# A recurrent block with a mixture of experts: the last expert's order, the residual loads and the closing additions

## The chip, the cores and the metric

The kernel runs on one core of a Trainium2 chip. The core has a matrix engine (PE, whose weight loads are listed apart as PEld), a vector engine (DVE), a scalar engine (ACT), GpSimd (POOL), a queue engine that here only issues DMAs (SP), and 16 DMA engines. The metric is the device time of one execution in microseconds (us). Times inside an execution are counted from the start of its span, that is, from the first to the last instruction.

## The reference

The input is x, 8192 tokens of 256 float32 values. What is computed, cut to what matters here:

```python
xn = layernorm(x)                       # per token
s  = recurrent(xn)                      # linear, gate, scan over time, linear: 8192 x 256
# mixture of experts on the same xn: 32 experts, 4 per token, at most 1280 tokens per expert
h   = silu(xe @ w1[e]) * (xe @ w3[e])   # xe: the tokens that were sent to expert e
out = (h @ w2[e]) * weight              # per slot
y   = zeros.at[token].add(out)          # scatter-add back to the tokens
z   = (silu(xn @ sw1) * (xn @ sw3)) @ sw2
return x + s * silu(y + z)
```

All of it is float32.

## The kernel before

**First stage (to about 390 us).** The tokens are taken in 8 rounds of 1024. Per round x is normalised, transposed, routed (top 4 of 32 experts by way of group maxima), projected by the recurrent part into `s_all`, which stays in SBUF (16 chunks of 128 partitions x 4 rows x 256), and sent row by row to the experts' slots in the DRAM table `xd_d` by indirect DMAs of POOL (`send`, L437). Two operations of this stage appear in the prediction: `recur` (L326), where DVE runs a scan over 8 x 1024 elements with two SBUF inputs (L333), and `scale` (L265), where POOL computes a power on 128 x 8 elements (L275). The shared expert z is computed here as well and stored to the DRAM table `y_d`.

**Expert stage (about 400 to 1226 us).** An expert's 1280 slots fall into three spans: two of 512 and a last one of 256. `load_slots` (L566) fetches a span from `xd_d`; `turn` (L576) transposes it on PE and computes the token numbers on DVE; `hidden` (L594, through `glu_hidden`, L113) does two matmul groups per half, a silu on ACT (L123) and a multiply on DVE (L124); `expert_out` (L597) multiplies by w2 on PE (L614), scales by the routing weight on ACT into `ob` (L617), and has POOL add each block of 128 rows to `y_d` by an indirect DMA with addition (L620, called a scatter below). `last_span` (L629) does the span of 256 under a condition: PE, DVE, ACT and POOL each load a flag and branch over it when an expert has no more than 1024 tokens.

The order on PE, DVE, ACT and SP is the program's own order (`manual_schedule`, L560); POOL is not among these engines, and its order is set by the scheduler, which puts the fourth scatter of span 0 behind the conditional span's two. The loop over experts (L646) is skewed: round e transposes and starts expert e while it finishes expert e - 1. One further round, e = 32, has no new expert; there only expert 31 is finished:

```python
            if old:
                hidden(e - 1, 1)
                expert_out(e - 1, 0)
            ...
            if old:
                last_span(e - 1)
            ...
            if old:
                expert_out(e - 1, 1)
```

Scatters of one expert go to different rows and do not wait for each other; the first of an expert waits until the last of the expert before it has landed.

**The residual chunks.** `load_residual` (L640) fetches a chunk of x into a tile `xr`. Thirteen of the sixteen are fetched in the expert stage, one after every second expert, into the pool `fin`. The other three are fetched after the stage into the pool `tail`, which takes over the SBUF space of the expert stage and so has to wait for the tiles that lay there.

**The tail (L671 on).** SP issues the 16 loads of `y_d` (y, 512 KB each). They need all scatters landed. Then for every chunk: a silu on ACT (L680), a multiplication by `s_all` on DVE (L681), an addition to `xr` on DVE (L682), and a store by SP (L683). SP issues its DMAs in program order over eight semaphores, and each DMA waits for the eighth before it to land; so the first store is issued when the ninth y load has landed.

Of the kernel before, what the change touches and what calls it, by code (L numbers as in the profile page):

```python
# [8 lines left out]
F32 = mybir.dt.float32  # L9
I32 = mybir.dt.int32  # L10
AF = mybir.ActivationFunctionType
ALU = mybir.AluOpType
# [4 lines left out]
def recurrent_moe_kernel(  # L17
# [18 lines left out]
    nc = tc.nc  # L36
    P = 128
    B, S, D = x.shape
# [12 lines left out]
    CT = 4  # L51
    CW = CT * P
    NC = N // CW
# [15 lines left out]
    out_f = out.rearrange("b s d -> (b s) d")  # L69
# [21 lines left out]
    s_all = keep.tile([P, NJ, D], F32, name="s_all")  # L91
# [5 lines left out]
    def apart(key, ins):  # L97

        tc.declare_no_dep(ins.ins, group=key, reason="different rows")
        tc.add_to_no_dep_group(key, ins.ins)  # L100

    def chunk(rows, c):

        r, h = divmod(c, RT // CT)
        return rows[r * TR : (r + 1) * TR, :].rearrange("(p j) d -> p j d", j=RT)[:, h * CT : (h + 1) * CT, :]

    def load_expert(e):
        w = wpool.tile([P, 3, KD, H], F32, tag="w", name=f"w_{e}")
        for i, src in enumerate((w1, w3, w2)):
            nc.sync.dma_start(out=w[:, i], in_=src[e].rearrange("(k p) h -> p k h", p=P))  # L110
        return w
# [15 lines left out]
    def transpose_in(src, j, p0, p1):  # L127

        for k, ps in enumerate((p0, p1)):
            nc.tensor.transpose(ps[:, j * P : (j + 1) * P], src[:, k * P : (k + 1) * P], ident)  # L130
# [4 lines left out]
    with tc.tile_pool(name="ab", bufs=1) as ab, tc.tile_pool(name="xp", bufs=4) as xp, tc.tile_pool(  # L135
        name="rt", bufs=2
# [31 lines left out]
        for i, src in enumerate((sw1, sw3, sw2)):  # L168
# [16 lines left out]
            out=tri, in_=tri, compare_op=ALU.is_gt, fill=0.0, base=0, pattern=[[1, P]], channel_multiplier=-1  # L185
# [18 lines left out]
            out=y_d[N : N + CAP, :].rearrange("(i p) d -> p i d", p=P),  # L204
            in_=hole[:, 0:D].unsqueeze(1).to_broadcast([P, EJ, D]),
# [293 lines left out]
        for r in range(NR + 1):  # L499
            new, old = r < NR, r > 0  # L500
            c = 2 * (r - 1)
# [54 lines left out]

    spans = [(i, min(CW, CAP - i)) for i in range(0, CAP, CW)]
    LAST = len(spans) - 1
    NX = NC - 3
    with tc.tile_pool(name="fin", bufs=NX, reuse_waits="tile") as fin, tc.manual_schedule(  # L560
        engines=engines
    ), ExitStack() as stack:
        mp = stack.enter_context(tc.tile_pool(name="moe", bufs=2, reuse_waits="tile"))
        ws, xes, rows, xTs, hTs = {0: first_w}, {}, {}, {}, {}

        def load_slots(e, i):  # L566
            s0, n = spans[i]
            xe = xes[e, i] = mp.tile(
                [P, n // P, XR], F32, tag=f"xe{n}", bufs=4 if n == CW else 2, name=f"xe_{e}_{s0}"
            )  # L570
            for j in range(n // P):
                q = s0 // P + j
                row0 = nc.sync.value_load(start[0:1, e, q : q + 1], min_val=FIRST - P, max_val=FIRST + E * EP - P)
                nc.sync.dma_start(out=xe[:, j, :], in_=xd_d[bass.ds(row0, P), :])

        def turn(e, i):  # L576

            s0, n = spans[i]
            m, j0 = n // P, s0 // P
            xe = xes[e, i]  # L580
            p0 = ps_tp.tile([P, CW], F32, tag="tp", name=f"ep0_{e}_{s0}")
            p1 = ps_tp.tile([P, CW], F32, tag="tp", name=f"ep1_{e}_{s0}")
            for j in range(m):
                transpose_in(xe[:, j, :], j, p0, p1)
            xT = xTs[e, i] = mp.tile([P, KD, n], F32, tag=f"xT{n}", name=f"xT_{e}_{s0}")
            nc.vector.tensor_copy(xT[:, 0, :n], p0[:, :n])  # L586
            nc.vector.tensor_copy(xT[:, 1, :n], p1[:, :n])  # L587
            row_f = mp.tile([P, CT], F32, tag="row_f", name=f"rf_{e}_{s0}")
            nc.vector.tensor_copy(row_f[:, :m], dump[:, j0 : j0 + m])
            nc.vector.copy_predicated(row_f[:, :m], used[:, e, j0 : j0 + m], xe[:, :m, XR - 1])  # L590
            row = rows[e, i] = mp.tile([P, CT], I32, tag="row", bufs=4, name=f"row_{e}_{s0}")
            nc.vector.tensor_copy(row[:, :m], row_f[:, :m])  # L592

        def hidden(e, i):  # L594
            hTs[e, i] = glu_hidden(mp, ws[e][:, 0], ws[e][:, 1], xTs.pop((e, i)), spans[i][1], f"{e}_{i}")

        def expert_out(e, i):  # L597

            s0, n = spans[i]
            w, xe, row, hT = ws[e], xes.pop((e, i)), rows.pop((e, i)), hTs.pop((e, i))  # L600
            ob = mp.tile([P, CT, D], F32, tag="ob", bufs=3, name=f"ob_{e}_{s0}")
            for j0 in range(0, n // P, 2):
                if n == CW:
                    po = ps_o.tile([P, 2, D], F32, tag="o", name=f"eo_{e}_{s0}_{j0}")
                    pos = [po[:, i, :] for i in range(2)]
                    order = [(m, i) for i in range(2) for m in range(KH)]
                else:
                    pos = [
                        ps_o.tile([P, 2, D], F32, tag="o", name=f"eo_{e}_{s0}_{j0 + i}")[:, 0, :] for i in range(2)
                    ]  # L610
                    order = [(m, i) for m in range(KH) for i in range(2)]
                for m, i in order:
                    tk = slice((j0 + i) * P, (j0 + i + 1) * P)
                    nc.tensor.matmul(pos[i], hT[:, m, tk], w[:, 2, m, :], start=(m == 0), stop=(m == KH - 1))  # L614
                for i in range(2):
                    j = j0 + i
                    nc.scalar.activation(ob[:, j, :], pos[i], AF.Copy, scale=xe[:, j, D + e : D + e + 1])  # L617
                    apart(
                        f"y{e}",
                        nc.gpsimd.indirect_dma_start(  # L620
                            out=y_d,
                            out_offset=bass.IndirectOffsetOnAxis(ap=row[:, j : j + 1], axis=0),
                            in_=ob[:, j, :],
                            in_offset=None,
                            compute_op=ALU.add,
                        ),
                    )

        def last_span(e):  # L629
            if (e, LAST) in xes:  # L630
                _, (more,) = nc.values_load_multi_w_load_instructions(  # L631
                    last[0:1, 0, e : e + 1], engines=(ET.PE, ET.DVE, ET.Activation, ET.Pool), min_val=0, max_val=1
                )
                with tc.If(more > 0):
                    hidden(e, LAST)
                    expert_out(e, LAST)

        xr = [None] * NC

        def load_residual(c, pool):  # L640
            xr[c] = pool.tile([P, CT, D], F32, tag="xr", name=f"xr_{c}")
            nc.sync.dma_start(out=xr[c], in_=chunk(x_f, c))

        for i in range(LAST + 1):
            load_slots(0, i)
        for e in range(E + 1):  # L646
            new, old = e < E, e > 0
            if new:
                turn(e, 0)
            if old:  # L650
                hidden(e - 1, 1)
                expert_out(e - 1, 0)
            if e + 1 < E:
                load_slots(e + 1, 0)
            if old:
                last_span(e - 1)
            if new:
                turn(e, 1)
                hidden(e, 0)
                turn(e, LAST)  # L660
            if old:
                expert_out(e - 1, 1)
            if e + 1 < E:
                ws[e + 1] = load_expert(e + 1)
                for i in range(1, LAST + 1):
                    load_slots(e + 1, i)
            if e % 2 == 1 and e // 2 < NX:
                load_residual(e // 2, fin)


        stack.close()  # L671
        tail = stack.enter_context(tc.tile_pool(name="tail", bufs=NC - NX, reuse_waits="tile"))
        for c in range(NX, NC):
            load_residual(c, tail)
        ys = []
        for c in range(NC):
            ys.append(tail.tile([P, CT, D], F32, tag="y", bufs=NC, name=f"y_{c}"))
            nc.sync.dma_start(out=ys[c], in_=chunk(y_d, c))
        for c, y in enumerate(ys):
            nc.scalar.activation(y, y, AF.Silu)  # L680
            nc.vector.tensor_tensor(y, y, s_all[:, c * CT : (c + 1) * CT, :], ALU.mult)  # L681
            nc.vector.tensor_tensor(xr[c], xr[c], y, ALU.add)  # L682
            nc.sync.dma_start(out=chunk(out_f, c), in_=xr[c])  # L683
# [1 line left out]
_INS = [  # L685
    "L0_attn_x",
# [35 lines left out]
```

## Time and profile before

| what | value |
|---|---|
| median of 3 runs | 1286.86 us (1284.95 to 1288.59) |
| the profiled execution: its time | 1286.5 us |
| the profiled execution: its span | 1284.8 us |
| mean granted PE clock | 0.958 |
| busy: PE | 1168.0 us (91%) |
| busy: DVE | 500.1 us (39%) |
| busy: ACT | 357.5 us (28%) |
| busy: POOL | 721.8 us (56%) |
| expert stage, 400 to 1226 us: PE busy | 812.5 us of 826.0 |
| from the last matmul to the first y load, 1226.0 to 1236.6 us: POOL busy | 7.2 us of 10.6 |
| tail, 1236.6 to 1284.8 us: DVE busy | 37.9 us of 48.2 |
| tail: DMA share, rate | 0.88, 348 GB/s |

The busy shares are averages over stages with different limits. The first two stages belong to PE; after 1226 us PE does nothing more, and 58.8 us of the span lie behind its last matmul. All that the change touches lies in or shortly before that end. A row of the timeline gives the start, the duration, the engine, the line, the operation and its tiles, and in brackets how long the engine was idle before it and what ended that idle time. In the chain of waits, each line is a piece of the work that ended last, in order of time: start, duration, engine, tile and line. Times on PE are modelled at the ends, and "issue" is time in which an engine waited for nothing that the profile shows.

### The profile page before, as it was taken

The numbers are of one execution on the slowest core, as the hardware profiler recorded it, in microseconds if no ns is written. First come the engines' busy times: TensorE is split into PE (matmuls) and PEld (weight loads), VectorE is DVE, ScalarE is ACT, GpSimd is POOL, SyncE is SP. The second block draws the span as 40 slices with busy tenths as digits, with TensorE's granted clock in tenths as the row PEclk, the third lists the DMA queues.
The fourth block names the chain that finished last, engine by engine and source line by source line (L and its number), as shares of the span: only waits on it lengthen the run. The fifth ranks groups of instructions, "written<-read, shape, count | busy, mean of one in ns | idle before, by whom it ended". The sixth has DMA issues, their size and how long they took to land. (4 is left out here: it accounts for less than half of the span.)

```text
span 1284.8 us, 15849 instructions
## 1 busy us (share of the span) xinstructions
PE 1168.0 (91%) x4246; PEld 733.7 (57%) x4246; DVE 500.1 (39%) x1591; ACT 357.5 (28%) x638; POOL 721.8 (56%) x561
## 2 busy tenths in 40 slices
PE   5599999999994999999999999999999999999910
PEld 3256565656552566666666656666666655665610
DVE  5765667564601322322223222332323232332238
ACT  2034433443320222222222222222222222222232
POOL 2477777777772355655545455545555545555630
PEclk9599999999996999999999999999999999999965
DMA  6134543433475476775776776758666767667488
GB/s 219 51 123 160 176 167 120 168 140 132 144 264 176 111 158 137 133 144 114 166 141 137 148 161 141 148 123 185 138 137 149 163 137 170 141 125 170 66 241 347
DMA packets 151251, 198.30 MB, mean 154 GB/s; under 512 B 17866, under 2 KB 134771, under 8 KB 151155
## 3 DMA queue, kind: packets, MB, share of 16 engines
q0 software_dynamic: 53184, 75.14, 30.8%
q1 hardware_dynamic: 95280, 120.01, 30.2%
q10 hardware_dynamic: 2690, 2.04, 0.5%
q8 instruction: 38, 0.62, 0.2%
q14 instruction: 59, 0.48, 0.1%
HBM read 99.05 MB, written 98.08 MB: 153 GB/s over the span
## 5 line engine op out<-in xcount | busy, mean ns | idle before, releaser
L620 POOL DMA_INDIRECT y_d<-ob,row x284 | 440.0, 1549 | 396.3 <-ACT ob L617 332.9
L440 POOL DMA_INDIRECT xd_d<-xt,put x256 | 263.7, 1030 | 94.0 <-issue 75.6
L95 PE MATMUL pa<-xT,w 128*128 128x512 f32 (+1 forms) x624 | 271.1, 557 | 0.0
L95 PE MATMUL pb<-xT,w 128*128 128x512 f32 (+1 forms) x624 | 269.3, 554 | 0.0
L614 PE MATMUL eo<-w,hT 128*128 128x256 f32 x1136 | 258.1, 379 | 0.1
L614 PEld LDWEIGHTS eo<-w,hT 128*128 128x128 f32 x1136 | 212.4, 190 | 42.9 <-issue 15.3
L617 ACT ACTIVATE ob<-eo,xe 128x256 f32<-128x256 f32 x284 | 120.0, 470 | 274.1 <-PE eo L614 229.7
L95 PEld LDWEIGHTS pb<-xT,w 128*128 128x128 f32 x624 | 118.7, 190 | 125.8 <-issue 122.9
L123 ACT ACTIVATE a<-pa 128x512 f32<-128x512 f32 (+1 forms) x156 | 87.2, 559 | 356.2 <-PE pa L95 343.0
L95 PEld LDWEIGHTS pa<-xT,w 128*128 128x128 f32 x624 | 114.2, 191 | 95.3 <-issue 92.4
L124 DVE TENSOR_TENSOR hT<-a,pb 128x512 f32<-128x512 f32 (+1 forms) x156 | 97.1, 638 | 162.2 <-PE pb L95 96.2
L592 DVE CAST row<-rf 128x4 int32<-128x4 f32 (+1 forms) x96 | 16.5, 172 | 270.7 <-DMA y_d<-ob,row 268.0
L586 DVE COPY xT<-ep 128x512 f32<-128x512 f32 (+1 forms) x96 | 57.6, 600 | 161.0 <-PE ep L130 161.0
L130 PE MATMUL ep<-ident,xe 128*128 128x128 f32 x640 | 89.7, 278 | 24.6 <-DMA xe<-xd_d 17.6
L130 PEld LDWEIGHTS ep<-ident,xe 128*128 128x128 f32 x640 | 75.0, 142 | 55.9 <-DMA xe<-xd_d 19.8
L95 PE MATMUL po<-Wio,xnT 128*128 128x256 f32 x256 | 71.7, 404 | 0.0
L95 PE MATMUL pa_s<-xnT,sw 128*128 128x512 f32 x128 | 61.0, 599 | 0.0
L95 PE MATMUL pb_s<-xnT,sw 128*128 128x512 f32 x128 | 60.2, 592 | 0.0
L95 PE MATMUL pz<-sw,hT_s 128*128 128x256 f32 x256 | 59.5, 385 | 0.4 <-DVE hT_s L124 0.4
L587 DVE COPY xT<-ep 128x512 f32<-128x512 f32 (+1 forms) x96 | 56.7, 591 | 0.0
L95 PEld LDWEIGHTS po<-Wio,xnT 128*128 128x128 f32 x256 | 45.3, 194 | 17.4 <-issue 13.8
L95 PE MATMUL po<-Wo_s,Si 9*128 9x256 f32 x128 | 54.7, 507 | 0.0
(124 smaller groups left out, 736.7 us busy)
## 6 DMA issues: line engine op xcount, KB each, us to landing
xe<-xd_d SPq DMA_DIRECT2D x320, 144.5 KB
w<-in_L_ffn_w_dram SPq DMA_DIRECT2D x96, 256.0 KB
xt<-in_L_attn_x_dram SPq DMA_DIRECT2D x16, 512.0 KB
y_d<-zt SPq DMA_DIRECT2D x16, 512.0 KB
xr<-in_L_attn_x_dram SPq DMA_DIRECT2D x16, 512.0 KB
y<-y_d SPq DMA_DIRECT2D x16, 512.0 KB
out_dram<-xr SPq DMA_DIRECT2D x16, 512.0 KB
xd_d<-hole SPq DMA_DIRECT2D x32, 144.5 KB
```

Source lines behind the costliest of these rows:

```text
L95: nc.tensor.matmul(ps, lhsT, rhs, start=(i == 0), stop=(i == len(pairs) - 1))
L123: nc.scalar.activation(a[:, :n], pa[:, :n], AF.Silu)
L124: nc.vector.tensor_tensor(hT[:, m, :n], a[:, :n], pb[:, :n], ALU.mult)
L130: nc.tensor.transpose(ps[:, j * P : (j + 1) * P], src[:, k * P : (k + 1) * P], ident)
L440: nc.gpsimd.indirect_dma_start(out=xd_d, out_offset=bass.IndirectOffsetOnAxis(ap=index, axis=0), in_=rows, in_offset=None,),
L586: nc.vector.tensor_copy(xT[:, 0, :n], p0[:, :n])
L587: nc.vector.tensor_copy(xT[:, 1, :n], p1[:, :n])
L592: nc.vector.tensor_copy(row[:, :m], row_f[:, :m])
L614: nc.tensor.matmul(pos[i], hT[:, m, tk], w[:, 2, m, :], start=(m == 0), stop=(m == KH - 1))
L617: nc.scalar.activation(ob[:, j, :], pos[i], AF.Copy, scale=xe[:, j, D + e : D + e + 1])
L620: nc.gpsimd.indirect_dma_start(out=y_d, out_offset=bass.IndirectOffsetOnAxis(ap=row[:, j : j + 1], axis=0), in_=ob[:, j, :], in_offset=Non ...
```

## The change

Four things are changed, all in the last block of the kernel.

1. In the round e = 32, expert 31's output of span 0 and its conditional span come ahead of the hidden part of span 1. For all other experts the order stays.
2. All 16 residual chunks are fetched in the expert stage (experts 27, 29 and 31 get one more each); the pool `fin` has 16 buffers, and the pool `tail` only holds the y chunks.
3. The first and the last chunk of the tail are done in two halves of 2 rows each: silu, multiplication, addition and store.
4. The addition of chunks 2, 5, 8 and 11 is done by POOL instead of DVE.

```diff
-    NX = NC - 3
-    with tc.tile_pool(name="fin", bufs=NX, reuse_waits="tile") as fin, tc.manual_schedule(
+    with tc.tile_pool(name="fin", bufs=NC, reuse_waits="tile") as fin, tc.manual_schedule(
...
-        def load_residual(c, pool):
-            xr[c] = pool.tile([P, CT, D], F32, tag="xr", name=f"xr_{c}")
+        def load_residual(c):
+            xr[c] = fin.tile([P, CT, D], F32, tag="xr", name=f"xr_{c}")
             nc.sync.dma_start(out=xr[c], in_=chunk(x_f, c))
...
+            if old and new:
+                hidden(e - 1, 1)
             if old:
-                hidden(e - 1, 1)
                 expert_out(e - 1, 0)
             if e + 1 < E:
                 load_slots(e + 1, 0)
             if old:
                 last_span(e - 1)
+            if not new:
+                hidden(e - 1, 1)
...
-            if e % 2 == 1 and e // 2 < NX:
-                load_residual(e // 2, fin)
+            if e % 2 == 1:
+                load_residual(e // 2)
...
-        tail = stack.enter_context(tc.tile_pool(name="tail", bufs=NC - NX, reuse_waits="tile"))
-        for c in range(NX, NC):
-            load_residual(c, tail)
+        tail = stack.enter_context(tc.tile_pool(name="tail", bufs=NC, reuse_waits="tile"))
...
         for c, y in enumerate(ys):
-            nc.scalar.activation(y, y, AF.Silu)
-            nc.vector.tensor_tensor(y, y, s_all[:, c * CT : (c + 1) * CT, :], ALU.mult)
-            nc.vector.tensor_tensor(xr[c], xr[c], y, ALU.add)
-            nc.sync.dma_start(out=chunk(out_f, c), in_=xr[c])
+            n = CT // 2 if c in (0, NC - 1) else CT
+            for j in range(0, CT, n):
+                yj, xj, sj = y[:, j : j + n, :], xr[c][:, j : j + n, :], s_all[:, c * CT + j : c * CT + j + n, :]
+                nc.scalar.activation(yj, yj, AF.Silu)
+                nc.vector.tensor_tensor(yj, yj, sj, ALU.mult)
+                adder = nc.gpsimd if c % 3 == 2 and c < NC - 4 else nc.vector
+                adder.tensor_tensor(xj, xj, yj, ALU.add)
+                nc.sync.dma_start(out=chunk(out_f, c)[:, j : j + n, :], in_=xj)
```

More of the change, by code (lines that the diff above doesn't have):

```diff
@@ L666, in recurrent_moe_kernel @@
                     load_slots(e + 1, i)
-            if e % 2 == 1 and e // 2 < NX:
-                load_residual(e // 2, fin)
+            if e % 2 == 1:
+                load_residual(e // 2)
         stack.close()
-        tail = stack.enter_context(tc.tile_pool(name="tail", bufs=NC - NX, reuse_waits="tile"))
-        for c in range(NX, NC):
-            load_residual(c, tail)
+        tail = stack.enter_context(tc.tile_pool(name="tail", bufs=NC, reuse_waits="tile"))
         ys = []
         for c in range(NC):
-            ys.append(tail.tile([P, CT, D], F32, tag="y", bufs=NC, name=f"y_{c}"))
+            ys.append(tail.tile([P, CT, D], F32, tag="y", name=f"y_{c}"))
             nc.sync.dma_start(out=ys[c], in_=chunk(y_d, c))
         for c, y in enumerate(ys):
-            nc.scalar.activation(y, y, AF.Silu)
-            nc.vector.tensor_tensor(y, y, s_all[:, c * CT : (c + 1) * CT, :], ALU.mult)
-            nc.vector.tensor_tensor(xr[c], xr[c], y, ALU.add)
-            nc.sync.dma_start(out=chunk(out_f, c), in_=xr[c])
+            n = CT // 2 if c in (0, NC - 1) else CT
[6 more added lines that the diff above has]
+                nc.sync.dma_start(out=chunk(out_f, c)[:, j : j + n, :], in_=xj)
 _INS = [
```

## The prediction

> **What bounds the kernel now.** Everything the change touches lies behind 1205 us of the span, so I read only the end. First the page's busy shares by slice: PE at 9 until slice 38, then near nothing. Then the chain of waits of the last 100 us, the timeline of POOL there, the busy time in stretches of 3 us, and last, from the first stage, the few places where POOL and DVE work on SBUF at once.
>
> The chain leaves PE at 1216 us, runs through POOL's scatters, the landing of the last one, the first y load, one silu, and then through DVE alone:
>
> ```profile
> 1232.85 3.72 DMA y_d<-ob,row
> 1236.58 4.15 DMA y<-y_d
> 1240.81 1.07 ACT y L680
> 1241.90 1.24 DVE y L681
> ...
> 1279.07 1.22 DVE xr L682
> ```
>
> So two things set the end: when the last scatter starts (1232.85), and DVE's 32 operations of 16 chunks, 1241.90 to 1280.29, 38.4 us, 2.40 a chunk.
>
> POOL's scatters of the last expert (columns: start, duration, then the idle time before it and its releaser):
>
> ```profile
> 1210.49 1.55 POOL L620 DMA_INDIRECT y_d<-ob,row  x1 [0.30 <-issue]
> 1215.25 1.55 POOL L620 DMA_INDIRECT y_d<-ob,row  x1 [3.21 <-ACT ob L617]
> ...
> 1221.73 1.55 POOL L620 DMA_INDIRECT y_d<-ob,row  x1 [1.22 <-ACT ob L617]
> ...
> 1227.29 1.55 POOL L620 DMA_INDIRECT y_d<-ob,row  x1 [0.30 <-issue]
> ```
>
> Ten scatters in a row, the last at 1232.85, at a pitch of 1.855 with two gaps, 3.21 at the front and 1.22 (0.92 over the usual 0.30). The seventh, at 1227.29, is the first of the second span: ACT had its copy at 1223.59 + 0.42, so it waited about 3.0 us in POOL's queue, not for data.
>
> The tail by stretches (PE, PEld, DVE, ACT, POOL busy, granted clock, DMA share, GB/s):
>
> ```profile
> 1239.00:1242.00 3.00, 0.00 (x0) 0.00 (x0) 0.10 (x1) 1.06 (x1) 0.00 (x0) 0.50 0.97 373
> ...
> 1272.00:1275.00 3.00, 0.00 (x0) 0.00 (x0) 2.97 (x3) 0.00 (x0) 0.00 (x0) 0.50 1.02 418
> 1275.00:1278.00 3.00, 0.00 (x0) 0.00 (x0) 2.97 (x4) 0.00 (x0) 0.00 (x0) 0.50 0.65 264
> 1278.00:1281.00 3.00, 0.00 (x0) 0.00 (x0) 2.26 (x2) 0.00 (x0) 0.00 (x0) 0.50 0.43 175
> 1281.00:1284.00 3.00, 0.00 (x0) 0.00 (x0) 0.00 (x0) 0.00 (x0) 0.00 (x0) 0.50 0.43 175
> ```
>
> DVE is full, but the DMA engines are full too, from 1239 to 1275, at up to 425 GB/s. Only the last 8 us are DVE's alone. That caps what a faster DVE can bring.
>
> **The order of the last expert.** PE's work is the same, moved: the output of span 0 comes straight after expert 30's (1205.87, its hT ready since 1202.8) instead of at 1212.74, then the conditional span (taken: eight matmuls more in the trace), then the hidden part and output of span 1. PE is gapless to 1219.5 and at clock 1.00, so span 1's output lands where it did, plus one new stall: its second hT half now ends right before it (the multiply, 0.69, and its start against 0.86 of matmuls that can go first; I take 0.7 with the waits, as the conditional span's own output shows 0.56 over 24 matmuls: 5.74 against 24 x 0.216). First copy 1223.59 + 0.7, first scatter ready 1225.0. POOL's queue keeps its order (three scatters of span 0, the conditional's two, the fourth, then span 1's four). It is free at 1212.04 and no longer idles for 3.21; the built instruction list puts the wait for expert 30's last scatter on the second of them. That one, issued 1210.49, lands 3.5 (least) to 4.7 (median) later, 1214.0 to 1215.2; counting on from there at 1.855, POOL reaches span 1 at 1223.3 to 1224.5, before its data. So the last scatter starts at 1225.0 + 3 x 1.855 = 1230.6: **2.3 gained**. Ends: 0.9 if the first one still starts at 1215.25 (only the gap at 1221 goes), 2.9 without the stall. Late next: ACT's copy of span 1.
>
> **The three residual loads.** One was already issued at 1189.96, two at 1226, beside the scatters. Now they go behind the slot loads of experts 27, 29 and 31, as thirteen did before. PE is busy 19.6 to 20.0 of every 20 us from 440 to 1220, with these loads (until 1070) and without, so I take 0; at most 0.4 lost, and at most 0.2 gained, since the last scatter landed in 3.73 and none in under 3.5. SP has nothing behind the last one until the y loads, and the three chunks are added only after 1271.
>
> **Halves of chunks 0 and 15.** DVE starts after half a silu: 1.06 against 0.60 of a 128x512 silu (L123), 0.46 earlier. Four half operations at 0.65 (L124's 0.686 less overlap) instead of 2.40: +0.2 a chunk, +0.4. The last store is half as long: 262 KB at 418 GB/s, 0.6 less. SP issues 18 stores at 0.33, hidden under transfers.
>
> **Four additions on POOL** (chunks 2, 5, 8, 11). Each takes 1.25 off DVE's pitch: 5.0. DVE's stretch becomes 38.4 - 5.0 + 0.4 = 33.8. POOL's price is not in the trace: per element, the select of 128x128 (0.293, less 0.103 for one element) gives 1.5 ns with one input, the iota of 1x320 (1.127) 3.2 ns. For 1024 elements that is 1.6 to 3.4 us; with two inputs I take 2.5. Three chunks last 6.0 on DVE, so POOL keeps up. The new wait: SP's store of such a chunk waits for POOL, all later stores are queued behind it, and only the end waits for those; chunk 11 leaves 12 to 15 (about 10 us) to catch up. But do POOL and DVE run side by side? The nearest rows are in the first stage:
>
> ```profile
> 174.81 2.34 DVE L333 TENSOR_TENSOR_SCAN Si<-Gt,Si,Si 8x1024 f32<-8x1024 f32 x1
> ...
> 175.92 2.22 POOL L440 DMA_INDIRECT xd_d<-xt,put  x1 [0.30 <-issue]
> ```
>
> ```profile
> 212.53 1.85 POOL L275 TENSOR_TENSOR rstd<-rstd,nhalf 128x8 f32<-128x8 f32 x1
> ...
> 212.89 0.42 DVE L427 TENSOR_TENSOR pos<-pos,eoff 128x256 f32<-128x256 f32 x1
> ```
>
> The scatter at 175.92 takes 2.22 instead of 0.96: it ends 0.99 after the scan with two SBUF inputs that began before it. POOL waits for DVE; the scan has its usual 2.34. In the other direction, DVE's operations at 212.89 and (L429) 213.34, two SBUF inputs each, have their usual 0.42 and 0.61 while POOL's elementwise operation runs to 214.38. It has 8 elements a partition, so it reads briefly; for 1024 the rows leave open a hold h on DVE between 0 and the addition's length, 0 to 3.4. I take the observed 0 for DVE, and up to 1.2 of waiting for POOL, which the 6.0 cover.
>
> [...]
>
> **The sum.** DVE's side of the tail gives 5.0 - 0.4 + 0.46 + 0.6 = 5.7. The DMA side gives less: after 1275 there remain 3 x (264 + 175 + 175) = 1842 KB, 4.4 us at 418 GB/s, so 1279.4 for the last byte against 1282.3 to 1284 now; I take 3.5 (2.9 to 4.6). The smaller counts: **2.3 + 3.5 = 5.8**. Span 1284.8 - 5.8 = 1279.0; the profiled execution took 1286.5, 1.7 around its span, and the median is 1286.86, 0.36 above it: **1281.1**, -0.45%. About 0.3% (3.9 us) is what a measurement can tell from no change.
>
> **Rivals.**
> - *POOL holds DVE* (the other side). If an addition keeps DVE out for h, DVE binds again and the change is -2.3 - 0.46 - 0.6 + 0.4 - 5.0 + 4h, about -8.0 + 4h. For it: the scan row shows exclusive use, and DVE has no slack from 1241.9 on. Against: the rows at 212. It turns slower at h = 2.0; h = 2.5 gives +2.0, 1288.9; above 3.0 it is slower by over 0.3%, at 3.4 by 5.6, 1292.5.
> - *Half a hold* (they share, h about 1.2): -3.2, 1283.7.
> - *The order brings only 0.9*, a wait for landing in place of the wait for ACT: -4.4, 1282.5. For it: 1215.25 is 4.76 after the last scatter, just the median landing.
> - *DMA does not bind* (stores drain more smoothly than now): 2.3 + 5.7 = 8.0, 1278.9. Against: a share of 1.0 for 36 us.
>
> **How the numbers follow.** Side by side (with the third and fourth rival as its edges, -4.4 to -8.0) 0.50; half a hold 0.14; a full hold 0.30, of which 0.12 above h = 3.0; something else on POOL that starves the stores 0.06. The forecast is the first: 1281.1, its own range 1278.9 to 1282.5. The range over all cases goes from 1278.9 to 1290.0 (a hold of 2.8) and leaves out 0.20 (0.14 for longer holds, 0.06 for starved stores). Faster by over 0.3%: most of the first and a third of the second, 0.52; slower 0.12 + 0.06 = 0.18; within 0.30.
>
> **What would show it.** Order: the first y load issued near 1234.3 and the gap of 3.21 gone. POOL: additions of 1.6 to 3.4. DVE: every row of 128x1024 still 1.22; rows 2 us longer, four of them, mean a hold. DMA: share 1.0 nearly to the end. What would make it wrong: mostly h.

## The result, and the profile after

The changed kernel takes 1286.56 us (median of 14 runs, 1282.24 to 1289.29) against 1286.82 for the kernel before (14 runs on the same chip, 1282.84 to 1289.36). The ratio is **0.9999 [0.9983, 1.0014]**: no change that can be measured. The forecast was 1281.1, clearly faster. The profiled execution has a span of 1284.4 us, before 1284.8. So the four edits moved the span by 0.4 us, and the question is what became of the 5.8 that the prediction had promised.

Read the chain of waits of the changed kernel first (start, duration, engine, tile and line):

```profile
1229.82 3.82 DMA y_d<-ob,row
1233.78 4.20 DMA y<-y_d
1238.00 0.64 ACT y L684
1238.66 0.70 DVE y L685
...
1254.06 3.26 DVE xr L687
...
1262.02 3.24 DVE xr L687
...
1279.95 0.69 DVE xr L687
```

The front has moved as it should: the last scatter starts 3.0 us sooner than at 1232.85, the first y load 2.8 sooner than at 1236.58, and DVE starts at 1238.66 instead of 1241.90. Yet DVE ends at 1280.64, before at 1280.29. All that was gained in front is given back within DVE's stretch. Every DVE operation on a whole chunk took some 1.22 before; now there are rows of 3.26 and 3.24 among them.

POOL's queue at the last expert (start, duration, idle time before it and releaser) shows the new order at work:

```profile
1210.18 1.55 POOL L619 DMA_INDIRECT y_d<-ob,row  x1 [0.30 <-ACT ob L616]
1212.04 1.55 POOL L619 DMA_INDIRECT y_d<-ob,row  x1 [0.30 <-issue]
1214.29 1.55 POOL L619 DMA_INDIRECT y_d<-ob,row  x1 [0.71 <-DMA y_d<-ob,row]
...
1224.26 1.55 POOL L619 DMA_INDIRECT y_d<-ob,row  x1 [1.00 <-ACT ob L616]
...
1229.82 1.55 POOL L619 DMA_INDIRECT y_d<-ob,row  x1 [0.30 <-issue]
```

The gap of 3.21 is gone. The wait for expert 30's last scatter is still there, as 0.71 at 1214.29, and one wait for ACT's copy of span 1 is left, 0.70 over the usual 0.30.

Now the rows around the first addition that POOL does (chunk 2), from the timeline:

```profile
1243.72 2.35 DVE L685 TENSOR_TENSOR y<-y,s_all 128x1024 f32<-128x1024 f32 x2
...
1245.08 3.20 POOL L687 TENSOR_TENSOR xr<-xr,y 128x1024 f32<-128x1024 f32 x1 [13.71 <-DVE y L685]
1246.11 3.26 DVE L687 TENSOR_TENSOR xr<-xr,y 128x1024 f32<-128x1024 f32 x1
...
1249.29 1.21 DVE L685 TENSOR_TENSOR y<-y,s_all 128x1024 f32<-128x1024 f32 x1
```

The first row is a pair, the products of chunks 2 and 3; the pair ends at 1246.07 with no delay. POOL's addition starts at 1245.08, while the second product runs, and ends at 1248.28. DVE's next operation, the addition of chunk 3, starts at 1246.11 and needs 3.26 instead of 1.22: it ends at 1249.37, 1.09 after POOL. So the rows read as follows: POOL first waited some 1.0 us for the DVE operation in flight, worked for the other 2.2, and DVE's next operation stood still until it was done. The hold h, the time by which an addition on POOL keeps DVE out, is 3.26 - 1.22 = 2.04. The trace has four such DVE rows (3.26, 3.26, 3.24, 3.24), one for each of POOL's four additions (3.20, 3.21, 3.20, 3.25). In all four, POOL ends 2.19 to 2.21 after the DVE operation in flight, and DVE's next operation ends 1.08 to 1.09 after POOL.

What this does to the DMA engines stands in the stretches of 3 us (PE, PEld, DVE, ACT, POOL busy, granted clock, DMA share, GB/s):

```profile
1266.00:1269.00 3.00, 0.00 (x0) 0.00 (x0) 2.96 (x4) 0.00 (x0) 0.13 (x1) 0.50 1.02 416
1269.00:1272.00 3.00, 0.00 (x0) 0.00 (x0) 2.97 (x2) 0.00 (x0) 3.00 (x1) 0.50 0.51 209
1272.00:1275.00 3.00, 0.00 (x0) 0.00 (x0) 2.96 (x3) 0.00 (x0) 0.12 (x1) 0.50 0.69 274
1275.00:1278.00 3.00, 0.00 (x0) 0.00 (x0) 2.97 (x4) 0.00 (x0) 0.00 (x0) 0.50 0.63 250
1278.00:1281.00 3.00, 0.00 (x0) 0.00 (x0) 2.58 (x4) 0.00 (x0) 0.00 (x0) 0.50 0.67 262
1281.00:1284.00 3.00, 0.00 (x0) 0.00 (x0) 0.00 (x0) 0.00 (x0) 0.00 (x0) 0.50 0.24 90
```

The prediction had the share at 1.0 nearly to the end. It falls at 1269, six microseconds sooner than before: the loads are through, and DVE finishes chunks too slowly to feed the stores. In the row from 1269 DVE is "busy" for 2.97 with two operations where others have four; a busy share doesn't tell work from standing still, the count beside it does.

### The profile page after: what moved, and what is told of

It is laid out like the page before. It is cut to its first block, busy times and chain, and to the rows that moved or that the text cites. A ratio compares the mean times of both kernels' runs of the same rounds, so it can differ in the third digit from the quotient of the medians.

```text
span 1284.4 us, 15860 instructions
## 1 busy us (share of the span) xinstructions
PE 1165.9 (91%) x4246; PEld 733.1 (57%) x4246; DVE 503.6 (39%) x1591; ACT 358.0 (28%) x640; POOL 737.2 (57%) x565
## 3 DMA queue, kind: packets, MB, share of 16 engines
q10 hardware_dynamic: 2690, 2.04, 0.5%
```

## The experiments

**The measure.** The total time of one kernel differs by up to 6.5 us from run to run (1282.84 to 1289.36 for the kernel before). Much of that arises in the first 400 us, whose code is the same in every kernel here: in ten of the eleven profiles the first transposition of expert 0 comes at 396.7 to 402.0, in that of e9 at 571.1. The expert stage (from that transposition to the point below) has 799.1 to 800.6 in all profiles. So each profile is also read from a fixed point on: b, the first matmul of expert 30's output of span 1. T is the time from b to the end of the span. T falls into four parts, all taken from the trace: the issue of the first y load; from there to DVE's first product; DVE's stretch from that to its last operation; and from there to the end.

| kernel | b | y load issued | to first product | DVE's stretch | to the end | T |
|---|---|---|---|---|---|---|
| before | 1202.25 | 34.33 | 5.32 | 38.39 | 4.46 | 82.50 |
| after | 1201.94 | 31.84 | 4.88 | 41.98 | 3.78 | 82.48 |
| e1_no_pool | 1202.00 | 31.74 | 4.97 | 38.94 | 3.76 | 79.42 |
| e2_pool_only | 1199.71 | 34.39 | 5.12 | 41.47 | 4.45 | 85.44 |
| e3_one_sbuf | 1197.48 | 31.87 | 4.75 | 36.83 | 3.75 | 77.20 |
| e4_pe_add | 1196.30 | 31.65 | 4.85 | 36.35 | 4.48 | 77.33 |
| e5_order_only | 1201.49 | 32.80 | 5.23 | 38.42 | 4.04 | 80.49 |
| e6_resid_only | 1200.53 | 34.41 | 5.08 | 38.41 | 4.47 | 82.37 |
| e7_pool_seven | 1199.91 | 31.73 | 4.82 | 44.30 | 3.78 | 84.64 |
| e8_psum_no_pool | 1200.22 | 31.84 | 4.86 | 42.69 | 3.53 | 82.92 |
| e9_one_sbuf_six | 1370.24 | 31.75 | 4.80 | 33.90 | 6.82 | 77.27 |

After against before: -2.49, -0.44, +3.59, -0.68, together -0.02.

Each T comes from one profile. How well it repeats can be seen where the code is the same: the y load is issued at 31.65 to 31.87 in the seven kernels with both the new order and the moved residual loads, and at 34.33 to 34.41 in the three with the old order. The medians of the total, set against the kernel before on the same chip, agree with T for e1 (-2.99, T -3.08) and e2 (+2.60, T +2.94); for e3 (-7.62, T -5.30), e4 (-3.58, T -5.17), e5 (-1.03, T -2.01) and e9 (-2.13, T -5.23) they agree in sign and not in size.

**The theories.** Hold: each POOL addition keeps DVE out for about 2.04, more than the 1.25 it saves, and all else of the change works nearly as forecast. Against it: the gain in front was never there or the tail is bound by the DMA engines in any case, and the long DVE rows only fill time in which DVE would have waited.

### e1: the change without POOL's additions

```diff
-                adder = nc.gpsimd if c % 3 == 2 and c < NC - 4 else nc.vector
+                adder = nc.vector
```

> The changed kernel with all additions on DVE; the rest of the change stays. Times are compared as the last stretch of the profile, from the first matmul of expert 30's last output to the end of the span: 82.5 us before, 82.4 us with the change. Theory (POOL's addition keeps DVE out): the four DVE rows of about 3.25 us go back to 1.22, which takes off 4 x 2.04 and gives back 4 x 1.25, so 3.2 us less than with the change: 79.3. Rival (the DMA engines bind the tail, whatever DVE does, so POOL's additions were neither gain nor loss): 82.4, with the DMA share at 1.0 to the end.

Measured: 1281.36 us against 1284.35 of the kernel before on the same chip, 0.9977 [0.9967, 0.9987], and T 79.42, 3.08 less than before. The groups by form in the tail (count, then busy time, mean ns of one, and idle time before them), first of the changed kernel:

```profile
L687 DVE TENSOR_TENSOR xr<-xr,y 128x1024 f32<-128x1024 f32 x10 | 20.3, 2035 | 0.3
L685 DVE TENSOR_TENSOR y<-y,s_all 128x1024 f32<-128x1024 f32 x14 | 16.7, 1216 | 0.0
...
L687 POOL TENSOR_TENSOR xr<-xr,y 128x1024 f32<-128x1024 f32 x4 | 12.9, 3217 | 27.9 <-DVE y L685 23.1 <-issue 4.7
```

then of e1:

```profile
L687 DVE TENSOR_TENSOR xr<-xr,y 128x1024 f32<-128x1024 f32 x14 | 17.1, 1225 | 0.5
L685 DVE TENSOR_TENSOR y<-y,s_all 128x1024 f32<-128x1024 f32 x14 | 17.1, 1220 | 0.0
```

Ten additions take DVE 20.3 us beside POOL, fourteen take it 17.1 without. With four moved away, the ten that are left cost more than all fourteen did. The mean of 2035 ns hides it by mixing six rows of 1.22 with four of 3.25, so a mean far from every known duration should be taken apart. With POOL's additions gone, the order, the residual loads and the halves bring 3.08: this is what the change hid.

### e2: the kernel before with POOL's additions alone

```diff
-            nc.vector.tensor_tensor(xr[c], xr[c], y, ALU.add)
+            adder = nc.gpsimd if c % 3 == 2 and c < NC - 4 else nc.vector
+            adder.tensor_tensor(xr[c], xr[c], y, ALU.add)
```

> The kernel before with nothing but the additions of chunks 2, 5, 8 and 11 moved to POOL. Theory (hold): four DVE additions of about 3.25 us behind four POOL additions; the last stretch is 4 x (2.04 - 1.25) = 3.2 us longer than before, 85.7. Rival (POOL's additions run beside DVE and something else of the change costs what they bring): 3.5 us shorter, 79.0.

Measured: 1286.95 against 1284.35, 1.0025 [1.0015, 1.0035]; T 85.44, 2.94 more than before. DVE's stretch grows by 3.08, in the same rows as above:

```profile
L683 DVE TENSOR_TENSOR xr<-xr,y 128x1024 f32<-128x1024 f32 x12 | 22.8, 1900 | 0.4
...
L683 POOL TENSOR_TENSOR xr<-xr,y 128x1024 f32<-128x1024 f32 x4 | 12.9, 3215 | 27.7 <-DVE y L681 18.2 <-issue 9.5
```

By 4 x (2.04 - 1.25) it would be 3.16. The hold does not depend on the other parts: with all of them and with none, four additions on POOL cost 3.06 (82.48 - 79.42) and 2.94. So the rival, that something else of the change costs what POOL brings, falls.

### e3: the same additions on POOL, DVE with one SBUF input

The silu is written to PSUM and the product reads it there; where DVE adds, the product goes to PSUM too. So each DVE operation has one input in PSUM and one in SBUF. A PSUM tile of this kernel holds 512 elements a partition, so all 16 chunks are worked in halves. POOL's four additions are those of the change.

```diff
-                nc.scalar.activation(yj, yj, AF.Silu)
-                nc.vector.tensor_tensor(yj, yj, sj, ALU.mult)
-                adder = nc.gpsimd if c % 3 == 2 and c < NC - 4 else nc.vector
-                adder.tensor_tensor(xj, xj, yj, ALU.add)
+                aj = in_psum(c, j, "a")
+                nc.scalar.activation(aj, yj, AF.Silu)
+                pj = yj if on_pool else in_psum(c, j, "b")
+                nc.vector.tensor_tensor(pj, aj, sj, ALU.mult)
+                if not on_pool:
+                    nc.vector.tensor_tensor(xj, pj, xj, ALU.add)
...
+            if on_pool:
+                nc.gpsimd.tensor_tensor(xr[c], xr[c], y, ALU.add)
```

> The changed kernel, but silu writes to PSUM in halves and DVE's products for its own additions go to PSUM too, so that no DVE operation of the tail has more than one input in SBUF; POOL still adds chunks 2, 5, 8 and 11. DVE has 56 operations of 128x512 at about 0.65, 36.4 us. Theory in its narrow form (POOL's reads and a second SBUF input of DVE share one way): no DVE row over 0.7, POOL's additions near 2.2 without waiting, last stretch 82.5 - 2.8 (order) - 0.5 - 0.6 - 2.0 = 76.6. Rival (POOL's addition keeps DVE out whatever DVE reads): four rows near 2.7, last stretch 84 to 85.

Measured: 1276.73 against 1284.35, 0.9945 [0.9932, 0.9958]; T 77.20, 5.30 less than before and 0.6 over what was expected. The groups by form in the tail:

```profile
L693 DVE TENSOR_TENSOR xr<-by,xr 128x512 f32<-128x512 f32 x24 | 16.6, 692 | 0.8
...
L697 POOL TENSOR_TENSOR xr<-xr,y 128x1024 f32<-128x1024 f32 x4 | 9.4, 2352 | 26.4 <-DVE y L691 22.2 <-DMA out_dram<-xr 4.2
```

and the rows around the second of them:

```profile
1247.15 0.69 DVE L691 TENSOR_TENSOR by<-ay,s_all 128x512 f32<-128x512 f32 x1
1247.36 2.35 POOL L697 TENSOR_TENSOR xr<-xr,y 128x1024 f32<-128x1024 f32 x1 [4.16 <-DVE y L691]
1247.87 0.69 DVE L693 TENSOR_TENSOR xr<-by,xr 128x512 f32<-128x512 f32 x1
1248.48 0.69 DVE L691 TENSOR_TENSOR by<-ay,s_all 128x512 f32<-128x512 f32 x1
...
1249.20 0.69 DVE L693 TENSOR_TENSOR xr<-by,xr 128x512 f32<-128x512 f32 x1
```

The hold is gone on both sides. No DVE row is over 0.7, though four of them overlap each of POOL's additions, and POOL's addition takes 2.35 instead of 3.20 to 3.25: that is its price beside a DVE that doesn't disturb it, and the 0.85 to 0.90 more in the changed kernel was waiting. Two things differ from the changed kernel: where DVE's inputs lie, and that its operations are halves. No run has halves with two SBUF inputs beside POOL's addition, so the place of the inputs is not separated from the size by an experiment of its own. Against the size speaks a row of the kernel before, shown below: there POOL's operation of L275, begun beside a DVE operation on only 128x256 with two SBUF inputs, took 1.85 instead of 1.64 to 1.69. The stretches at the end of this kernel:

```profile
1266.00:1269.00 3.00, 0.00 (x0) 0.00 (x0) 2.90 (x6) 0.00 (x0) 0.00 (x0) 0.50 1.02 418
1269.00:1272.00 3.00, 0.00 (x0) 0.00 (x0) 1.89 (x3) 0.00 (x0) 0.00 (x0) 0.50 0.97 390
1272.00:1275.00 3.00, 0.00 (x0) 0.00 (x0) 0.00 (x0) 0.00 (x0) 0.00 (x0) 0.50 0.22 84
```

The DMA share is now near 1.0 to the end, as the prediction wanted it of the changed kernel. By the ratio to the kernel before this is the fastest kernel of all. Two remarks on its size. Its total is 7.6 us below the kernel before, T only 5.3; the rest lies outside T, where its code is that of the changed kernel, so I do not count it. And about 2.1 us lie around its span (1276.78 against 1274.7), 0.4 more than the 1.7 of before.

### e8: e3 with all additions on DVE

```diff
-            on_pool = c % 3 == 2 and c < NC - 4
+            on_pool = False
```

> The version with silu and products in PSUM, all additions on DVE. It shows what POOL's four additions are worth where they do not keep DVE out. Theory (they run beside DVE and take 8 operations of 0.65 off it): 5.2 more than the 77.2 with them, 82.4. Rival (the gain of that version came from PSUM operands or half operations, not from POOL): 77 to 78.

Measured: one run, 1284.96; T 82.92. This is the control for e3: PSUM operands with half operations bring nothing by themselves. On the contrary, they cost 3.50 against e1 (82.92 - 79.42): DVE's stretch is 42.69 against 38.94, since 64 half operations at a pitch of about 0.66 take longer than e1's 28 whole ones at 1.22 and 8 halves. The end of the tail starves the stores:

```profile
1269.00:1272.00 3.00, 0.00 (x0) 0.00 (x0) 2.93 (x5) 1.20 (x2) 0.00 (x0) 0.50 0.48 191
1272.00:1275.00 3.00, 0.00 (x0) 0.00 (x0) 2.90 (x6) 1.20 (x2) 0.00 (x0) 0.50 0.44 175
```

Between e8 and e3 only POOL's four additions differ (and the products that they read, which lie in SBUF), and they bring 5.72 (82.92 - 77.20). The same four additions lose 3.06 beside DVE operations with two SBUF inputs. One and the same edit has both signs, and what differs is where its neighbours read from (and, as said, that they are halves). Against e1, the way by PSUM and POOL together brings 2.22.

### e4: the four additions on PE

Each of the four sums is made by PE in PSUM as identity times `xr` plus identity times y. ACT copies it back, two chunks later in ACT's order.

```diff
-                adder = nc.gpsimd if c % 3 == 2 and c < NC - 4 else nc.vector
-                adder.tensor_tensor(xj, xj, yj, ALU.add)
+                if c % 3 == 2 and c < NC - 4:
...
+                        mm(ps, [(ident, xr[c][:, h : h + 2, :]), (ident, y[:, h : h + 2, :])])
...
+                nc.vector.tensor_tensor(xj, xj, yj, ALU.add)
```

> The changed kernel, with the additions of chunks 2, 5, 8 and 11 done by PE (two products with the identity, summed in PSUM) and copied out by ACT two chunks later; POOL does nothing in the tail. Theory (hold by POOL): DVE loses the same four additions without any hold, 33.8 us in all, and the DMA engines bind at the end: 2.8 (order) + 3.5 less than before, 76.2, DMA share 1.0 to the end. Rival (DVE is slowed by any second engine that works on the chunks, or SP's order starves the stores): 80 or more.

Measured: 1280.77 against 1284.35, 0.9974 [0.9963, 0.9985]; T 77.33. There is no long DVE row, so the rival, that any second engine at work on the chunks slows DVE, falls. DVE's stretch is 36.35, 2.59 under e1's. That is less than the 5.0 expected; nearly all of the rest, 2.36, is lost at one place:

```profile
1242.64 1.23 DVE L702 TENSOR_TENSOR xr<-xr,y 128x1024 f32<-128x1024 f32 x1
...
1244.66 0.59 ACT L683 COPY xr<-fo 128x512 f32<-128x512 f32 x1 [2.83 <-PE fo L95]
1245.14 2.95 ACT L691 ACTIVATE y<-y 128x1024 f32<-128x1024 f32 x3
1246.23 2.36 DVE L694 TENSOR_TENSOR y<-y,s_all 128x1024 f32<-128x1024 f32 x2 [2.36 <-ACT y L691]
```

PE had been idle for 18.7 us, and its granted clock from 1239 to 1245 is 0.50 (from 1248 to 1263 it is 1.00); two products in a row take 1.91 to 2.07 from 1239.13 to 1244.4, but 1.02 at 1248.47 and at 1249.33. ACT waits 2.83 for the second half of the sum, the silus of the next chunks stand behind that copy on ACT, and DVE waits 2.36 for them. T is within 0.13 of that of e3 all the same, and 1.1 over the 76.2 that was expected: something else sets the end by then, which e9 shows. T and the total do not agree in size here. T is 5.17 below before, the medians 3.58 apart; the profiled execution was the fastest of its seven (1275.88, the others 1279.3 to 1281.4). By the interval the kernel is faster than before; whether its tail is as good as e3's in every run is open.

### e9: e3 with six additions on POOL

```diff
-            on_pool = c % 3 == 2 and c < NC - 4
+            on_pool = c % 2 == 1 and c < NC - 4
```

> The version with silu and products in PSUM, with six additions on POOL (chunks 1, 3, 5, 7, 9, 11) instead of four. Theory (with the hold gone, the DMA engines bind the tail, whose share is 1.0 until the last store): DVE's stretch shrinks by 4 operations of 0.65 to 34.2, but the last stretch stays at 76.5 to 77.2. Rival (DVE still binds): 77.2 - 2.6 = 74.6.

Measured: 1449.1 against 1451.23, 0.9987 [0.9970, 1.0004]. On the chip of this comparison both kernels took some 170 us longer, and in the profile that lies in the first stage, so only T is set beside the other runs: 77.27, e3 77.20. DVE ends 3.0 us sooner than in e3 (70.45 against 73.45 after b), and the end does not come sooner:

```profile
1436.00:1439.00 3.00, 0.00 (x0) 0.00 (x0) 2.93 (x5) 0.00 (x0) 0.00 (x0) 0.50 1.02 418
1439.00:1442.00 3.00, 0.00 (x0) 0.00 (x0) 1.66 (x3) 0.00 (x0) 0.00 (x0) 0.50 1.02 418
1442.00:1445.00 3.00, 0.00 (x0) 0.00 (x0) 0.00 (x0) 0.00 (x0) 0.00 (x0) 0.50 0.99 397
1445.00:1448.00 3.00, 0.00 (x0) 0.00 (x0) 0.00 (x0) 0.00 (x0) 0.00 (x0) 0.50 0.10 36
```

DVE has nothing more to do from 1440.7 on, and the DMA engines are full until 1445. Here they alone set the end. e3, e4 and e9, whose DVE stretches are 36.83, 36.35 and 33.90, all have a T of 77.2 to 77.3: no way of unloading DVE that was tried goes below it.

### e5 and e6: the order alone, the residual loads alone

e5 is the kernel before with the two conditions of the order:

```diff
-            if old:
+            if old and new:
                 hidden(e - 1, 1)
+            if old:
                 expert_out(e - 1, 0)
...
+            if not new:
+                hidden(e - 1, 1)
```

> The kernel before with nothing but the new order of expert 31. Theory (the order alone moves the end of the scatters): the first y load is issued 31.8 us after the first matmul of expert 30's last output, as with the whole change, instead of 34.3; the last stretch is 2.5 us shorter than before, 80.0. Rival (part of this came from taking the residual loads away from the scatters): first y load at 33 or later, last stretch 81 or more.

e6 is the kernel before with all 16 residual chunks in the pool `fin`:

```diff
-            if e % 2 == 1 and e // 2 < NX:
-                load_residual(e // 2, fin)
+            if e % 2 == 1:
+                load_residual(e // 2)
...
-        for c in range(NX, NC):
-            load_residual(c, tail)
```

> The kernel before with nothing but the three residual loads moved into the expert stage. Theory: no difference, last stretch 82.5 within 0.4, and the expert stage (first transposition of expert 0 to expert 30's last output) 800.3 as before. Rival (the loads beside the scatters delayed the y loads): last stretch 81.5 or less; or the stage grows.

Measured: e5 1282.47 against 1283.5, 0.9991 [0.9978, 1.0004], T 2.01 below before; e6 one run, 1284.65, T 0.13 below before, which I count as nothing. By the total, e5 cannot be told from the kernel before. By T it lies between the two cases of its expectation: the y load at 32.80 comes later than the 31.8 of the theory, and T of 80.49 is 0.5 over its 80.0. In e5 the last scatter starts 27.88 after b, just as in the changed kernel and 2.72 sooner than before. But the y load comes 0.96 later than there. The chain of e5 shows why:

```profile
1229.37 4.90 DMA y_d<-ob,row
1234.29 4.12 DMA y<-y_d
```

The last scatter lands in 4.90 instead of 3.82. Two residual loads were issued between 1225.65 and 1226.50 and need a median of 6.9; in the new order they overlap the last scatter's transfer, which came later in the old one. That the residual loads make the difference is shown by the edits; that they do it by this overlap is read from the times of this one profile. So the two parts work together: the order alone brings 1.53 of the y load's issue, the residual loads alone -0.08, both 2.49.

### e7: seven additions on POOL

```diff
-                adder = nc.gpsimd if c % 3 == 2 and c < NC - 4 else nc.vector
+                adder = nc.gpsimd if c % 2 == 1 and c < NC - 1 else nc.vector
```

> The changed kernel with seven additions on POOL instead of four (chunks 1, 3, 5, 7, 9, 11, 13). Theory (each addition on POOL costs DVE 2.04 and saves it 1.25): last stretch 79.4 + 7 x 0.79 = 84.9, seven DVE rows near 3.25. Rival (the loss is a thing of single places, such as the last one at 1270, where the DMA share falls to 0.51): about 82.4, as with four.

Measured: one run, 1286.26; T 84.64, 5.22 more than e1. There are seven long DVE rows (3.24 to 3.27), and the first shows the pattern:

```profile
1240.49 3.20 POOL L687 TENSOR_TENSOR xr<-xr,y 128x1024 f32<-128x1024 f32 x1 [11.15 <-issue]
1241.51 3.26 DVE L687 TENSOR_TENSOR xr<-xr,y 128x1024 f32<-128x1024 f32 x1
```

The price grows with the count: 5.22 / 7 = 0.75 for one, 3.06 / 4 = 0.77 in the changed kernel, 0.79 by h - 1.25. Had the tail been bound by the DMA engines with DVE's long rows only filling waits, three more would have cost nothing, and a loss at single places would have left T near 82.4. Both fall.

## Why the prediction was wrong

**The step that failed** is the one on POOL: "for 1024 the rows leave open a hold h on DVE between 0 and the addition's length, 0 to 3.4. I take the observed 0 for DVE". The runs showed h of about 2.04 (2.02 to 2.05) in its place, in every one of the 15 additions of after, e2 and e7. The bounds were right, the value within them was not. The 0 was read from a POOL operation on 8 elements a partition, 128 times fewer than the addition's 1024; carrying it over to the addition was the author's estimate, which no row of the kernel before showed. The row did show a wait all the same, in POOL's own duration: 1.85 instead of 1.64 to 1.69. Here are that row and another of the same line, each with the DVE operation with two SBUF inputs that was in flight when it began:

```profile
212.43 0.43 DVE L426 SCALAR_TENSOR_TENSOR M<-pos,M 128x256 f32<-128x256 f32 x1
212.53 1.85 POOL L275 TENSOR_TENSOR rstd<-rstd,nhalf 128x8 f32<-128x8 f32 x1
...
300.11 1.21 DVE L330 SCALAR_TENSOR_TENSOR Si<-Gt,Si 8x1024 f32<-8x1024 f32 x1
300.93 1.93 POOL L275 TENSOR_TENSOR rstd<-rstd,nhalf 128x8 f32<-128x8 f32 x1
```

POOL does this operation eight times. The other six, with no such DVE operation in flight, take 1.64 to 1.69. So the row that was read as "no hold" had itself waited for DVE. The scan's row, in the prediction's fence ahead of that row, said the same: there too POOL took longer beside DVE's operation, 2.22 instead of 0.96. Whether DVE waits for POOL in the same way, these rows left open; the runs show that it does, with h = 2.04.

**The rival had it right.** "POOL holds DVE" was priced at -8.0 + 4h with its turn at h = 2.0. With 2.04 that gives +0.2; measured were -0.4 in the span and -0.02 in T. With this h the forecast's DVE stretch of 33.8 becomes 33.8 + 4 x 2.04 = 42.0, measured 41.98. No other term of that sum was off enough to matter. The result lies inside the range over all cases only because this case was part of it. "Half a hold" (h about 1.2) fails: no hold was under 2.02. The forecast gave side by side 0.50 and a full hold 0.30; one outcome does not measure a chance, but the scan's row spoke for the hold on its face, and the row at 212 did when compared with its like.

**The other steps:**
- *The order, 2.3.* Measured 2.49 (34.33 to 31.84), slightly under-sized. The last scatter starts 2.72 sooner: the stall taken at 0.7 for span 1's second half was smaller (PE stands idle for 0.42 there), and the first copy was ready for POOL at 1224.26 and not 1225.0 (0.31 of that is b). That 2.49 comes so near is partly luck, as the next point says: the order alone measured 1.53. The rival "the order brings only 0.9" fails: the wait for landing is 0.71, and the slack before span 1 absorbs it.
- *The residual loads, 0.* True in the old order (e6). In the new one it is a term of 1.0 (31.84 against 32.80 in e5), which the 2.3 contained without saying so. The prediction looked at what the loads would disturb in the place they move to; for the place they leave, it took the scatters' landing as it was in the old order.
- *The halves, 0.46 sooner, +0.4 on DVE, 0.6 at the end.* Measured after against before: 0.44, +0.55 (e1's 38.94 against 38.39) and 0.68. In e1 against e5 the same three terms are 0.26, +0.52 and 0.28, nothing in sum; so as an edit of their own they are not shown to bring anything.
- *POOL's addition, 2.5 with 1.6 to 3.4.* It is 2.35 undisturbed, 3.20 to 3.27 with the wait for DVE; "up to 1.2 of waiting for POOL" was 0.85 to 0.92.
- *The cap by the DMA engines.* Right, and only seen where DVE is relieved: e3's T is 5.30 below before, 2.46 of it in the y load's issue and 2.84 in the tail, against 3.5 forecast with 2.9 to 4.6, so just under its lower end. The rival "DMA does not bind" fails with e9.

So the forecast of -5.8 comes near e3 (-5.3), a kernel in which both engines do run side by side, rather than the one that was built. It does so by the bound of the DMA engines: DVE's stretch in e3 is 36.83 and not 33.8, since its half operations take back part of what POOL saves.

## What to carry to other kernels

Before an elementwise operation goes from DVE to POOL, look where DVE's neighbouring operations read. Here they took two inputs from SBUF, POOL read SBUF too, and each addition on POOL cost DVE 2.04 of POOL's 2.35 for the 1.25 that it saved; where the pattern is the same, price the off-load with such a hold until a run shows another. It pays only if the hold is shorter than what it saves. With an operand of DVE put into PSUM on the way, the same off-load brought 5.72 here; but the way by PSUM, with its half operations, had a price of its own, 3.50, which has to be taken off. And a hold of 2.04 by an operation on 1024 elements a partition was not refuted by a row whose operation has 8. When one engine's row shows nothing, compare the other engine's row with its like.

## What the runs showed of the hardware that was not expected

- An addition of 128x1024 float32 takes POOL 2.35 us beside DVE operations with one SBUF input, 1.9 times DVE's 1.22. Beside DVE operations with two SBUF inputs, it keeps DVE out for all but some 0.3 of that (h = 2.04).
- In all 15 additions of after, e2 and e7, POOL and DVE alternate where both have two SBUF inputs: the DVE operation in flight ends with its usual 1.21 to 1.22, POOL ends 2.19 to 2.22 after it, and DVE's next operation 1.08 to 1.09 after POOL. These constant distances fit engines that stand until the other is done, and not ones that share at half speed. POOL's addition quite alone, with DVE idle, was not tried.
- A POOL operation that starts while such a DVE operation runs takes longer: the addition by 0.85 where 0.99 of it was left (1245.08), in the kernel before the small operation of L275 by some 0.18 and 0.26 (against 1.67) where 0.32 and 0.39 were left.
- In the tail of e3, loads and stores together move at 404 to 423 GB/s in stretches of 3 us from 1239 to 1269, at a DMA share of 1.02 to 1.04; the T of e3, e4 and e9 lie within 0.15 us of each other at that bound.
- In e4's profile PE, idle for 18.7 us before 1239.13, was granted a clock of 0.50 from 1239 to 1245, 0.96 from 1245 to 1248 and 1.00 from 1248 to 1263.
- The end of the first stage varied by 5.3 us between ten profiles with the same code, and in that of e9 came some 170 us later, while the expert stage (799.1 there) and T (77.27) stayed as they were. All 29 runs of e9's comparison, of either kernel, had a mean granted clock of 0.897 to 0.907 and took 1443.56 to 1454.54 us; in those of e1 to e8 and their kernel before the clock was 0.955 to 0.970. Which of the two, the clock or the delay, is the cause of the other, or whether a third thing is behind both, these runs do not settle.
